# Mamba block of a fused graph network: six chunks of four tiles and one of two, with the first head in two halves

## The chip, the cores and the metric

The kernel runs on one core of a Trainium2 chip. The metric is the device time of one launch in microseconds (us). The engines are named as the profile names them: PE multiplies matrices (PEld is its weight load), DVE is VectorE, ACT is ScalarE, POOL is GpSimd, and SP issues DMAs.

## The reference

Four graph layers follow each other on 3327 nodes of 256 features, each with a residual and a layer norm. Layer 1 is the one that changes:

```python
h = relu(adj @ x @ gcn_w + gcn_b);  h = (h - mu) * rsqrt(var + EPS) * ln_g + ln_b
xz = h @ w_in;  xc, z = xz[:, :512], xz[:, 512:]
xconv = sum(xpad[k:k + L] * conv_w[:, k] for k in range(4)) + conv_b
u = silu(xconv);  dbc = u @ w_xp
dt = softplus(dbc[:, :16] @ w_dt + b_dt);  B = dbc[:, 16:32];  C = dbc[:, 32:]
dA = exp(dt[:, :, None] * A);  dBu = dt[:, :, None] * B[:, None, :] * u[:, :, None]
hst = dA[t] * hst + dBu[t];  ys[t] = hst @ C[t]      # a scan over the nodes, 512 channels x 16 states
out = ((ys + u * D_skip) * silu(z)) @ w_out
x = layernorm(x + out)
```

## The kernel before

The 3327 nodes are padded to 26 tiles of 128. Layer 0 comes first, then layer 1 (the Mamba block, some 350 to 1383 us of the profile), then layers 2 and 3, which the change leaves alone.

In the Mamba block, channels lie on partitions in four groups `g` (`NG`), and nodes run along the free dimension. The nodes are cut into chunks; `ends` and `starts` (from L263) hold their bounds. They are 3, 4, 4, 4, 4, 4 and 3 tiles, that is 384 columns in the first and last chunk and 512 in the others. Three streams of work are interleaved.

**Convolution.** `convolve` (L326) is a generator over the 26 tiles. A tile takes 26 matmuls against adjacency blocks loaded by SP (L340, L341), then a tail: ACT copies the sum to `m` (L349), PE transposes it (L352), ACT copies again (L354), PE multiplies by `gcn_w` (L357, L358), ACT applies relu (L361) and sums squares (L318), POOL makes the scale (L322 to L324), ACT applies it (`norm`, L368), PE turns the tile (`turn`, L378), and ACT writes it into `hT` (L380). A new tile's sum lies in the PSUM buffer `cb`, of which there is one, or for tiles 2, 4 and 6 in `y3`. `pump(tiles)` runs the generator until so many tiles are done.

**Head of a chunk.** The class `Head` (L483) makes what the scans read. `project` multiplies `hT` by `w_in` (L497), copies to `xc` (L499) and starts `u` (L500); `taps` adds three shifted products on DVE (L507); then `silu`, `mixed` (the product with `w_sp`, L521, whose rows B and C go to DRAM as `bc`, L526), `step_size` (L535 to L537), `exponentials`, `rounding`, `logarithms` and `finish`, which leaves dt and `du` (L560). A change between silu, exp and ln reloads ACT's table (`table_of`). `last` hands the last three columns from one head to the next.

**Scans.** For each chunk there are 16 slots, one for each state `s`. A slot takes, for each of four groups, a decay `dA` (ACT, two PSUM buffers, L600) and a scan (DVE, L615); then `product` (DVE, `hc`, two buffers) with the row C, and `add_up` (PE transposes into the accumulators `y0` to `y3`, L632), which is issued in the next slot. `feed` (POOL, L608) fills the next input of the scan from `du` and row B. `row` (L592) loads both rows from `bc`. Once `pinned` is set, DVE and POOL keep the program's order, and ACT's decays and table changes stand in one chain (`in_turn`, L289); the profile books DVE and POOL instructions of that part at L282, the line of the wrapper. The rest of PE's and ACT's work is placed by a scheduler, which prefers what stands under `tc.high_priority()`.

The head of chunk c + 1 and the output of chunk c - 1 are spread over the slots of chunk c: `plan(c)` gives the slot of each step, with slots of its own for chunk 0. The output is `gate` (DVE), `gated` (L643, L645) and `residual` (L656 to L661). `quota` sets how many units of convolution a slot may take. It spreads the tiles of chunk n evenly between two due times, by `duty`, an estimate of the slot's other PE work, and keeps `AHEAD` units in hand. In chunk 0 it gives nothing before slot 8. When all tiles are convolved, `values` prepares layer 2 in the same places: `value` transposes a finished tile (L460), copies it (L462), multiplies it by `wg` (L466) and writes `col` (L467) and `F` (L469, L470).

Before the slots stand `pump(3)`, the whole first head at 384 columns, and `pump(7)`. After the slots comes a tail over the last chunk's three tiles: add up, gate, transpose, `w_out` (L654), norm (L811), and their `value`. Layer 2 starts with a maximum over `col` (L923).

Of the kernel before, what the change touches and what calls it, by code (L numbers as in the profile page):

```python
# [18 lines left out]
P = 128  # L19
# [7 lines left out]
AHEAD = 96  # L27
SPLIT = 54
WC = 512
# [18 lines left out]
def gnn_kernel(ctx: ExitStack, tc: tile.TileContext, n: int, a: dict, out: bass.AP):  # L48
# [107 lines left out]
    with tc.tile_pool(name="l1b", bufs=1) as wpool, tc.tile_pool(name="l1at", bufs=2) as l1at:  # L156
# [35 lines left out]
        with tc.tile_pool(name="l1aw", bufs=1) as cwork, tc.tile_pool(name="l1c", bufs=2) as ch, \  # L192
# [61 lines left out]
            def plan(c):  # L254


                if c == 0:
                    return dict(project={g + 1: (g,) for g in range(NG)}, taps={7: (0,), 8: (1,), 9: (2, 3)}, gates={5: (0, 1), 6: (2,)},
                                silu=9, mixed=10, sizes={10: (0, 1), 11: (2, 3)}, exps=(11, 12), log=13)
                return dict(project={5: (0, 1), 6: (2, 3)}, taps={7: (0, 1), 8: (2, 3)}, gates={7: (0, 1), 8: (2, 3)},  # L260
                            silu=8, mixed=9, sizes={9: (0,), 10: (1, 2), 11: (3,)}, exps=(11, 12), log=13)

            ends = []  # L263
            while not ends or ends[-1] < npad:
                prev = ends[-1] if ends else 0
                ends.append(min(npad, prev + min(WC, (3 + len(ends)) * P)))
# [37 lines left out]
            banks = {0: ["y0", "y1", "y2", "ps"], 1: ["y3", "ps"]}  # L304
# [21 lines left out]
            def convolve():  # L326
# [3 lines left out]
                for it in range(nt):  # L330
                    if it < ends[1] // P and it % 2 == 0 and it:
                        cb = ypsum.tile([P, DI], F32, name="y3")
                    else:
                        cb = cpsum.tile([P, DI], F32, name="cb")
# [90 lines left out]
            def due(c):  # L425
                return c * DS + min(plan(c)["project"]) if c else 8
# [3 lines left out]
            def quota(c, s):  # L430


                k = c * DS + s
                n = next((x for x in range(2, nch) if k < due(x - 1)), None)
                if n is None:
                    return 24
                if k < due(0):
                    return 0
                if n not in shares:
                    busy = [duty(*divmod(i, DS)) for i in range(due(n - 2), due(n - 1))]  # L440
                    more = TILE * tiles_of(n)
                    level = max(busy) + more
                    while sum(max(0, level - x) for x in busy) > more:
                        level -= 1
                    shares[n] = [max(0, level - x) for x in busy]
                return TILE * starts[n] // P + sum(shares[n][:k - due(n - 2) + 1]) + AHEAD - taken
# [36 lines left out]
            class Head:  # L483

                def __init__(self, c):
                    self.c, self.w = c, ends[c] - starts[c]

                def project(self, g):

                    c, w = self.c, self.w  # L490
                    if g == 0:
                        self.xc = scratch()
                        gps.tensor_copy(self.xc[:, :, :3], last)
                        us[c] = ch.tile([P, NG, WC], F32, name="u", bufs=1)[:, :, :w]
                    ps = bank(self.c)
                    for k in range(2):
                        ten.matmul(ps[:, :w], w_in[:, k, g * P:(g + 1) * P], hTs[c][:, k, :w],  # L497
                                   start=(k == 0), stop=(k == 1))
                    act.copy(self.xc[:, g, 3:3 + w], ps[:, :w])  # L499
                    act.activation(us[c][:, g, :], self.xc[:, g, 0:w], AF.Identity, scale=conv_w[:, g, 0:1],  # L500
                                   bias=conv_b[:, g:g + 1])

                def taps(self, g):

                    u, w = us[self.c][:, g, :], self.w
                    for k in range(1, 4):
                        vec.scalar_tensor_tensor(u, self.xc[:, g, k:k + w], conv_w[:, g, k:k + 1], u,  # L507
                                                 op0=ALU.mult, op1=ALU.add)
                    if g == NG - 1:
                        gps.tensor_copy(last, self.xc[:, :, w:w + 3])  # L510

                def silu(self):
                    in_turn(act.activation, us[self.c], us[self.c], AF.Silu)

                def mixed(self):

                    c, w = self.c, self.w
                    m = w_sp.shape[2]
                    ps = bank(self.c)
                    for g in range(NG):  # L520
                        ten.matmul(ps[:m, :w], w_sp[:, g, :], us[c][:, g, :], start=(g == 0), stop=(g == NG - 1))  # L521
                    self.left = tmp.tile([P, WC], F32, name="gt", bufs=1)[:m, :w]
                    act.copy(self.left, ps[:m, :w])
                    bc = rows_of[c] = l1d.tile([2, DS, w], F32, name=f"bc{c}")
                    for k in range(2):
                        nc.sync.dma_start(bc[k], self.left[32 * k + DTR:32 * k + DTR + DS])  # L526
# [12 lines left out]
                def exponentials(self, g):  # L539

                    if g == 0:
                        self.e1 = scratch()[:, :, :self.w]
# [11 lines left out]
                def finish(self):  # L554

                    c, w, e1 = self.c, self.w, self.e1
                    vec.tensor_sub(e1, e1, self.e)
                    vec.scalar_tensor_tensor(e1, self.v, 0.0, e1, op0=ALU.max, op1=ALU.add)
                    du = ch.tile([P, NG, WC], F32, name="du", bufs=1)[:, :, :w]
                    vec.tensor_mul(du, e1, us[c])  # L560
                    xs[c] = e1, du
# [101 lines left out]
            pump(ends[0] // P)  # L663
            xs, ys = {}, {}
            first = Head(0)
            with tc.high_priority():
                for g in range(NG):
                    first.project(g)
                    first.taps(g)
                first.silu()  # L670
                table_of(AF.Exp)
                first.mixed()
                for g in range(NG):
                    first.step_size(g)
                for g in (0, 2):
                    first.exponentials(g)
                table_of(AF.Ln)
                first.rounding()
                first.logarithms()
                table_of(AF.Exp)  # L680
                first.finish()
            pump(ends[1] // P)
# [10 lines left out]
            for k, (c, s) in enumerate(states):  # L693
# [8 lines left out]
                if added:  # L702
                    with tc.high_priority() if s == 0 or c == 0 else nullcontext():
# [16 lines left out]
                if s == 0:  # L720
                    ys[c] = [ypsum.tile([P, DI], F32, name=f"y{i}") for i in range(m)]
                    with tc.high_priority() if c == 0 else nullcontext():
                        add_up(ys[c], us[c], first=True)
# [42 lines left out]
                if after:  # L766
                    if s == min(p["project"]):
                        pump(ends[c + 1] // P)
                    first = [lambda g=g: ahead.project(g) for g in p["project"].get(s, ())]
                    if s == p["mixed"]:  # L770
                        first += [ahead.mixed]
                    first += [lambda g=g: ahead.step_size(g) for g in p["sizes"].get(s, ())]
                    if c:
                        uses += first
                    else:
                        with tc.high_priority():
                            for use in first:
                                use()
# [844 lines left out]
```

## Time and profile before

| | us |
|---|---|
| three runs | 3509.28, 3515.73, 3515.77; median 3515.73 |
| the profiled execution | 3512.67, of which its span 3510.8 |
| chunk 0, from its first scan (436.60) to that of chunk 1 | 141.2 |
| chunks 1, 2, 3, 4 | 139.7, 139.4, 140.1, 138.9 |
| chunk 5, chunk 6 | 130.9, 95.2 |
| from the end of chunk 6's last scan (1361.95) to the maximum over `col` | 21.4 |

Times inside the profile are counted from the span's start. A line of an order of time gives start, length, engine, line of the kernel, operation, output and input with their shapes, and a count of merged instructions; the bracket at its end is the engine's idle time ahead of it and what ended that. A line of waits gives the waiting engine and tile, the releaser, the total in us, how many times, and the longest.

### The profile page before, as it was taken

The numbers are of one execution on the slowest core, as the hardware profiler recorded it, in microseconds if no ns is written. First come the engines' busy times: TensorE is split into PE (matmuls) and PEld (weight loads), VectorE is DVE, ScalarE is ACT, GpSimd is POOL, SyncE is SP. The second block draws the span as 40 slices with busy tenths as digits, with TensorE's granted clock in tenths as the row PEclk, the third lists the DMA queues.
The fourth block names the chain that finished last, engine by engine and source line by source line (L and its number), as shares of the span: only waits on it lengthen the run. The fifth ranks groups of instructions, "written<-read, shape, count | busy, mean of one in ns | idle before, by whom it ended". The sixth has DMA issues, their size and how long they took to land. (4 is left out here: it accounts for less than half of the span.)

```text
span 3510.8 us, 42847 instructions
## 1 busy us (share of the span) xinstructions
PE 3228.0 (92%) x15415; PEld 2526.5 (72%) x15415; DVE 2374.3 (68%) x5256; ACT 1737.1 (49%) x2749; POOL 932.2 (27%) x942
## 2 busy tenths in 40 slices
PE   9999888988988776999899999999997999999996
PEld 5888766666676555888677878777785777777775
DVE  2111168999999997777444444545434999999996
ACT  1000456767767674111233333333336888888883
POOL 0000055656665653111100000000001233333332
PEclk9999999999999888999899999999999999999998
DMA  5443334433443222444221212121212122222220
GB/s 179 147 151 122 112 104 115 113 106 118 101 115 90 67 58 92 131 142 149 84 67 49 65 48 67 50 64 53 61 48 73 55 57 69 66 69 61 70 66 16
DMA packets 138323, 304.62 MB, mean 87 GB/s; under 512 B 19086, under 2 KB 58574, under 8 KB 137966
## 3 DMA queue, kind: packets, MB, share of 16 engines
q1 hardware_dynamic: 138094, 301.72, 29.0%
q8 instruction: 125, 2.05, 0.2%
q14 instruction: 104, 0.85, 0.1%
HBM read 291.01 MB, written 10.65 MB: 86 GB/s over the span
## 5 line engine op out<-in xcount | busy, mean ns | idle before, releaser
L282 POOL TENSOR_TENSOR h<-du,row 128x2048 f32<-128x2048 f32 (+1 forms) x110 | 465.6, 4233 | 344.5 <-DVE hc L282 252.1
L282 DVE TENSOR_TENSOR_SCAN h<-dA,carry,h 128x512 f32<-128x512 f32 (+1 forms) x384 | 449.0, 1221 | 18.6 <-ACT dA L289 18.5
L289 ACT ACTIVATE dA<-t,A_log 128x512 f32<-128x512 f32 (+1 forms) x448 | 292.5, 658 | 146.3 <-DVE h L282 144.8
L1099 PE MATMUL acc<-X,wt 128*128 128x256 f32 x1352 | 346.3, 393 | 10.6 <-ACT wt L1097 10.2
L1066 PE MATMUL acc<-F,at 128*128 128x256 f32 x1352 | 354.3, 387 | 0.9 <-ACT q L840 0.6
L1099 PE MATMUL acc<-G,wt 128*128 128x256 f32 x1352 | 336.9, 392 | 5.5 <-ACT wt L1030 5.1
L1099 PEld LDWEIGHTS acc<-X,wt 128*128 128x128 f32 x1352 | 244.6, 191 | 106.2 <-issue 41.3
L1066 PE MATMUL acc<-X,at 128*128 128x256 f32 x1352 | 308.4, 381 | 0.0
L975 PE MATMUL acc<-F,at 128*128 128x257 f32 x1352 | 304.9, 382 | 1.3 <-DMA U<-in_U 1.3
L341 PE MATMUL cb<-F,at 128*128 128x256 f32 x1196 | 294.1, 394 | 4.8 <-ACT hn L361 3.4
L1099 PEld LDWEIGHTS acc<-G,wt 128*128 128x128 f32 x1352 | 250.7, 193 | 65.8 <-ACT wt L1030 35.2
L1111 DVE MAX8 cand<-e 128x8 f32<-128x128 f32 x676 | 142.2, 279 | 229.6 <-ACT e L1052 218.0
L118 PE MATMUL acc<-xa,at 128*128 128x257 f32 x1352 | 294.7, 380 | 0.0
L1066 PEld LDWEIGHTS acc<-F,at 128*128 128x128 f32 x1352 | 238.2, 191 | 75.3 <-issue 50.2
L118 PEld LDWEIGHTS acc<-xa,at 128*128 128x128 f32 x1352 | 255.9, 189 | 38.3 <-issue 0.5
L1066 PEld LDWEIGHTS acc<-X,at 128*128 128x128 f32 x1352 | 252.9, 191 | 40.3 <-issue 8.3
L975 PEld LDWEIGHTS acc<-F,at 128*128 128x128 f32 x1352 | 254.5, 191 | 37.3 <-issue 1.5
L632 PE MATMUL y<-ident,hc 128*128 128x128 f32 x1664 | 236.9, 297 | 46.2 <-DVE hc L282 46.1
L632 PEld LDWEIGHTS y<-ident,hc 128*128 128x128 f32 x1664 | 210.3, 154 | 87.5 <-DVE hc L282 62.8
L341 PEld LDWEIGHTS cb<-F,at 128*128 128x128 f32 x1196 | 229.4, 198 | 54.4 <-issue 14.5
L282 DVE TENSOR_TENSOR hc<-h,row 128x2048 f32<-128x2048 f32 (+2 forms) x114 | 242.3, 2127 | 11.0 <-PE y L632 4.3
L1097 ACT COPY wt<-tp 128x512 f32<-128x512 f32 (+1 forms) x182 | 93.6, 557 | 312.1 <-PE tp L1095 311.9
(351 smaller groups left out, 5219.4 us busy)
## 6 DMA issues: line engine op xcount, KB each, us to landing
at<-in_adjT SPq DMA_DIRECT2D x104, 832.0 KB, 4.5
at<-in_adjT SPq DMA_DIRECT2D x260, 320.0 KB, 3.0
row<-bc SPq DMA_DIRECT2D x80, 512.0 KB, 5.0
at<-in_adjT SPq DMA_DIRECT2D x52, 576.0 KB, 4.1
at<-in_adjT SPq DMA_DIRECT2D x26, 512.0 KB, 3.6
row<-bc SPq DMA_DIRECT2D x32, 384.0 KB, 4.8
qd<-q SPq DMA_DIRECT2D x104, 32.0 KB, 1.9
q<-qd SPq DMA_DIRECT2D x52, 64.0 KB, 1.9
```

Of the source, the lines that this page charges most:

```text
L118: nc.tensor.matmul(acc, at[:, j, :], rhs[:, j0 + j, :], start=(j0 + j == 0), stop=(j0 + j == nt - 1))
L282: return lambda *x, **k: tc.keep_in_program_order(op(*x, **k))
L289: decays.append(op(*x, **k))
L341: ten.matmul(acc, at[:, j % JC, :], X0[:, j, :], start=(j == 0), stop=(j == nt - 1))
L632: x = ten.matmul(y[:, g * P:(g + 1) * P], h[:, g, i * P:(i + 1) * P], ident, is_transpose=True, start=(first and g == 0), stop=(last and g ...
L975: nc.tensor.matmul(acc, at[:, j, :], F[:, j0 + j, :], start=(j0 + j == 0), stop=(j0 + j == nt - 1))
L1066: nc.tensor.matmul(acc, at[:, j, :], rhs[:, j0 + j, :], start=(j0 + j == 0), stop=(j0 + j == nt - 1))
L1097: copy(wt[:, :m, :], pt[:, :m, :])
L1099: nc.tensor.matmul(acc, wt[:, j, :], rhs[:, j0 + j, :], start=(j0 + j == 0), stop=(j0 + j == nt - 1))
L1111: nc.vector.max(cand[:, s * 8:(s + 1) * 8], z[:, s * SEG:(s + 1) * SEG])
```

## The change

The chunks become six of four tiles and one of two. The first head is made in two halves of 256 columns: `Head` takes an offset `o` and a width, and writes its part of `u`, `rows_of`, dt and `du`. Each half follows the convolution of its two tiles. Six tiles and not seven are convolved before the slots (`FREE`); tiles 6 and 7 are given to the slots 0 to 5 of chunk 0 by `quota`. The steps of chunk 1's head and the gates of chunk 0 move to other slots. In chunk 0 these steps and most `add_up` calls lose their high priority, and the head of chunk 1 the PSUM banks of its own.

```diff
+FREE = 6
 def plan(c):
     if c == 0:
-        return dict(project={g + 1: (g,) for g in range(NG)}, taps={7: (0,), 8: (1,), 9: (2, 3)}, gates={5: (0, 1), 6: (2,)},
+        return dict(project={6: (0, 1), 7: (2, 3)}, taps={8: (0, 1), 9: (2, 3)}, gates={8: (0, 1), 9: (2, 3)},
                     silu=9, mixed=10, sizes={10: (0, 1), 11: (2, 3)}, exps=(11, 12), log=13)
...
-    ends.append(min(npad, prev + min(WC, (3 + len(ends)) * P)))
+    ends.append(min(npad, prev + WC))
-banks = {0: ["y0", "y1", "y2", "ps"], 1: ["y3", "ps"]}
+banks = {0: ["y0", "y1", "y2", "ps"]}
...
-        if it < ends[1] // P and it % 2 == 0 and it:
+        if it in (2, 4):
             cb = ypsum.tile([P, DI], F32, name="y3")
...
 def due(c):
-    return c * DS + min(plan(c)["project"]) if c else 8
+    return c * DS + min(plan(c)["project"])
 def quota(c, s):
     k = c * DS + s
-    n = next((x for x in range(2, nch) if k < due(x - 1)), None)
+    n = next((x for x in range(1, nch) if k < due(x - 1)), None)
     if n is None:
         return 24
-    if k < due(0):
-        return 0
+    begin, tiles = (due(n - 2), starts[n] // P) if n > 1 else (0, FREE)
     if n not in shares:
-        busy = [duty(*divmod(i, DS)) for i in range(due(n - 2), due(n - 1))]
-        more = TILE * tiles_of(n)
+        busy = [duty(*divmod(i, DS)) for i in range(begin, due(n - 1))]
+        more = TILE * (ends[n] // P - tiles)
...
-    return TILE * starts[n] // P + sum(shares[n][:k - due(n - 2) + 1]) + AHEAD - taken
+    return TILE * tiles + sum(shares[n][:k - begin + 1]) + AHEAD - taken
 class Head:
-    def __init__(self, c):
-        self.c, self.w = c, ends[c] - starts[c]
+    def __init__(self, c, o=0, w=None):
+        self.c, self.w, self.o = c, w or ends[c] - starts[c], o
+        self.all = ends[c] - starts[c]
+    def mine(self, x):
+        return x[:, :, self.o:self.o + self.w]
...
-pump(ends[0] // P)
 xs, ys = {}, {}
-first = Head(0)
-with tc.high_priority():
-    for g in range(NG):
-        first.project(g)
-        first.taps(g)
+for o in range(0, WC, WC // 2):
+    pump((o + WC // 2) // P)
+    first = Head(0, o, WC // 2)
+    with tc.high_priority():
+        for g in range(NG):
+            first.project(g)
+            first.taps(g)
...
-pump(ends[1] // P)
+pump(FREE)
...
-        with tc.high_priority() if s == 0 or c == 0 else nullcontext():
+        with tc.high_priority() if s == 0 else nullcontext():
             summed = add_up(*added)
...
-        with tc.high_priority() if c == 0 else nullcontext():
-            add_up(ys[c], us[c], first=True)
+        add_up(ys[c], us[c], first=True)
...
-        first = [lambda g=g: ahead.project(g) for g in p["project"].get(s, ())]
+        uses += [lambda g=g: ahead.project(g) for g in p["project"].get(s, ())]
         if s == p["mixed"]:
-            first += [ahead.mixed]
+            uses += [ahead.mixed]
-        first += [lambda g=g: ahead.step_size(g) for g in p["sizes"].get(s, ())]
-        if c:
-            uses += first
-        else:
-            with tc.high_priority():
-                for use in first:
-                    use()
+        uses += [lambda g=g: ahead.step_size(g) for g in p["sizes"].get(s, ())]
```

The methods of `Head` read and write through `self.u`, `self.mine(...)` and the offset `o`, and the half with `o == 0` allocates the tiles that both halves share.

## The prediction

> **What bounds the kernel now.** I read the page's slices first, then busy time by stage, then VectorE's waits and its order of time. The page has DVE at 9 tenths and PE at 8 to 9 in slices 5 to 15, the Mamba block. The table of busy time by stage, cut at the first scan of each chunk (columns: stretch, its length, then PE, PEld, DVE, ACT and POOL busy, granted clock, DMA share, GB/s), says which chunk is bound by what:
>
> ```profile
> 436.60:577.80 141.20, 116.68 (x544) 87.37 (x542) 103.96 (x97) 88.07 (x176) 68.08 (x36) 0.94 0.38 109
> 577.78:717.50 139.72, 124.00 (x604) 95.38 (x605) 132.09 (x100) 96.50 (x187) 89.77 (x35) 0.93 0.39 110
> ...
> 996.93:1135.84 138.91, 119.52 (x619) 91.68 (x617) 132.99 (x101) 95.69 (x182) 86.13 (x32) 0.96 0.37 102
> 1135.84:1266.70 130.86, 93.31 (x446) 71.78 (x446) 128.53 (x101) 95.28 (x203) 76.57 (x24) 0.84 0.27 63
> 1266.70:1361.95 95.25, 67.81 (x348) 52.82 (x348) 88.38 (x85) 64.63 (x166) 54.38 (x18) 0.86 0.24 58
> ```
>
> From chunk 1 on DVE is busy 93 to 98%: the scans set the pace. Chunk 0 is the exception: 37 of its 141.2 us are idle on DVE though it has only three tiles. DVE's order of time shows where the largest piece lies:
>
> ```profile
> 479.66 3.49 DVE L282 TENSOR_TENSOR_SCAN h<-dA,h 128x384 f32<-128x384 f32 x4
> 500.07 2.33 DVE L282 SCALAR_TENSOR_TENSOR u<-t,conv_w,u 128x512 f32<-128x512 f32 x3 [16.91 <-ACT u L500]
> ```
>
> The taps of chunk 1's head stand in slot 7 of chunk 0 and wait 16.9 us for the projection, which waits for tile 6 (its hT is done at 494.65). DVE's waits of this stretch add the rest:
>
> ```profile
> DVE h L282 <- ACT dA L289: 20.9, 8, 5.9
> DVE u L282 <- ACT u L500: 16.9, 1, 16.9
> ```
>
> **What the skill says.** The Trainium skill, "VectorE: DVE Perf Modes", section on the TRN2 errata, gives (N+151)/0.96 ns for an fp32 tensor_tensor. The trace agrees: 1.76 us at 1536 elements, 2.29 at 2048. For 1024 I take its 1.22 us, an estimate. "ScalarE: Activation LUTs", section What ACT_TABLE_LOAD costs, gives 1283 ns for a table load, and the trace has 1.28; a second head pays four of them again. Its further drain of 1380 ns is not seen: after the load at 410.98 the next ACTIVATE starts at 412.28. Its 280 + 0.833 N ns for an ACTIVATE fits dA (0.582 us at 384 columns, 0.688 at 512) within 4%; I take 0.48 at 256. "Perfetto Trace Analysis", Identifying the Most-Contended Engine, warns that matmul busy time is no measure of headroom: PE at 0.89 of a full chunk is PEld at 0.68, but PE still waits 15 us in each for ACT's copies, so I treat PE as nearly full.
>
> **The change, part by part.** The order of the changed program's instructions, engine by engine, was read beside that of before. Prices: a four-tile slot is 4.80 us of scans (0.06 less each without carry) and 2.29 of product, 7.1 us in cadence, 6.85 without carry; a convolution step (a 256-wide fp32 matmul) is two PE instructions at 0.22 us each (48 in 10.55), so a tile is 11.5 us and about 2 for its tail; the 16 transposes of a slot are 2.65 us (12 in 1.98).
>
> 1. *Start of the scans.* Now: hT of tile 2 at 399.86, Ln of the head ends at 429.28, du at 434.65, first scan 436.60. After: the first half starts behind tile 1 (hT 385.72) and puts 16 projection instructions (3.5 us), 8 of w_sp (1.8), 8 of w_dt (0.8) and a wait for hn behind the last table load (2.8) into PE's queue, ahead of tiles 2 and 3. By PE's order tile 2 is convolved at 397.7, tile 3 at 415.9, its hT (7.6 us later, as for tile 1) at 423.4. The second half at 256 columns takes 22.8 us from there to the end of Ln, against 29.4 at 384 (two thirds of the copies, step sizes and exponentials, and Ln is no longer behind tile 3's norm): 446.1. Three DVE instructions at 1.22: du at 449.9; the first quarter of the 512-wide POOL feed 1.3: **first scan at 451.4, +14.8 us.** The extra two bc writes (0.4 us each on SP) and the halves' copies of last on POOL hide under this chain; with their cover gone they cost 1 us.
>
> 2. *Chunk 0, four tiles.* Its own DVE work is 16 x 6.85 + 17.9 (12 taps at 0.75, four 2048-wide steps) = 127.5 us. PE has tile 5 done at 453.6, as scanning begins, and the order puts tile 6 whole ahead of the first slot's transposes, 7 and 8 ahead of the sixth's. PE: 5 + 21 matmuls and the turn of tile 5 bring it to 471.4, the first slot's transposes with tile 6's tail to 477.4. The products have two buffers, so slot 2's product, ready at 471.0, waits to 477.6: 6.5 us. After that PE and DVE go side by side to slot 7 (513 to 515), with 2.7 us more of such waits and 1.4 at the start. The projection follows in slots 6 and 7 and is done at about 519 and 527, before the taps at 521 and 531: **the 16.9 us wait is gone.** Slots 8 to 15 are taken from chunk 1 of now (74.3 us from slot 8's product to the end, 1.8 less without carry). Sum 147 us against 141.2: **+5.8**, for one tile more. SP's queue: row loads stand ahead of at loads and wait for a product; by the same walk each at load still lands before its matmul (tile 8's last third by 506, wanted at 508), so I cost them nothing; if cover fails, 4.1 us each.
>
> 3. *Chunks 1 to 4* keep shapes and pacing. Four residuals in chunk 1 and not three is what chunk 2 has now, in 139.4 us. Chunk 4 convolves two tiles and not three: **-1.**
>
> 4. *Chunk 5* prepares a 256-wide head: 12 taps 0.15 us less each and four steps 1.76 to 1.22: **-3.9.** The gates moved to slots 8 and 9 are PE and ACT work, under DVE.
>
> 5. *Chunk 6, two tiles.* DVE's own work falls from 16 x 5.5 + 2.4 to 16 x 3.9 (4 x 0.67 + 1.2) + 2.4 = 65 us. But ACT, 64.6 us busy there now, keeps 58 (64 dA shorter by 0.10, one sz copy and half the silu less, one `value` of 1.2 more), in an order that mixes `value`, residual and gt into dA, with just two dA buffers and scans of 0.67. One `value` goes L460, m, L466, col, F and was 4.7 us long from 1344.69, above a slot's 3.9. Such ACT work already stalls at 384 columns:
>
> ```profile
> 1359.93 1.93 DVE L282 TENSOR_TENSOR_SCAN h<-dA,carry,h 128x384 f32<-128x384 f32 x2 [1.90 <-ACT dA L289]
> ```
>
>    Bounds: 68 (DVE's work, all hidden) and 90 (5.6 a slot). I take 82, so **-13.2.**
>
> 6. *Tail.* From the last product (1361.95) to the maximum over col (1383.33) 21.4 us for three tiles; the second tile's col stands at 1378.19, and the first product starts the same. One tile less: **-5.3.**
>
> Sum: 14.8 + 5.8 - 1 - 3.9 - 13.2 - 5.3 = **-2.8 us**. Against the profiled execution's 3512.67 that is 3509.9; the median shown is 3.06 above it. I say 3512.0, a fall of 0.1% from 3515.73. All else (layer 0, layers 2 and 3) is untouched. A measurement of this kernel can tell about 0.2%, 7 us, from no change.
>
> **The rivals.**
> - *The short last chunk runs at DVE's pace*, and the wait at slot 2 is all that PE costs chunk 0. For it: chunk 5 now has 0.9 us of dA waits with the same values; ACT was busy 65 of chunk 6's 95 us. Against: the four-link chain of a `value`. Chunk 6 at 70 and chunk 0 at 145 give -17: 3499.
> - *PE becomes the bound of chunk 0.* Three tiles and seven slots' transposes are 61 us of PE work in the 62 us to slot 7, with PE unstalled. In chunks 1 to 4 PE is 89% busy at best, because each tile's tail waits for two ACT copies that now queue behind dA. At 89% the 61 become 69, the debt reaches the projection and moves the taps of slots 8 and 9: +8 us, and 4 more in chunk 1, whose slots 6 and 7 already wait 4.3 us for the transposes. That gives +9: 3525. It decides when the first slot's transposes end after about 482. Against: at 480 to 506 PE ran with the full clock and few waits.
> - *It doesn't do what it says:* the scheduler could leave tiles 6 and 7 where they were. The order of the changed program excludes that; chance 1 in 100.
>
> **How the numbers follow.** The sum as it stands, with 3 us either way for the start, 6 for chunk 0 and 6 for chunk 6, holds 0.42; the first rival and cases like it 0.31; PE as the bound and other slower cases 0.26; no change of order 0.01. The likeliest case alone spans 3506 to 3519. The unknown ends (chunk 6 from 68 to 90, chunk 0 from 145 to 159) carry the range to 3499 and 3527. Of the 0.42 some 0.08 fall under -7 us and 0.03 over +7; of the 0.31 some 0.28 are under -7; of the 0.26 some 0.23 are over +7. So: faster 0.36, same 0.38, slower 0.26.
>
> **What would show it.** Right: first scan near 451; no DVE wait for u in slot 7 and one wait of 5 to 8 us of a product for the transposes in slot 2; chunk 0 of 147 us, the last chunk near 82, col's maximum about 16 us after the last product. Wrong: DVE waits for transposes through slots 3 to 9 (PE binds), a last chunk under 74 with no dA waits (first rival), or a first scan after 456.

## The result, and the profile after

The changed kernel takes 3509.88 us (median of 12 runs, 3504.62 to 3513.86). In the same series the kernel before took 3511.91 (12 runs, 3509.22 to 3515.97), so the ratio is 0.9994, with a 95% interval of 0.9985 to 1.0002: no difference that can be told. The profiled execution took 3504.92 us (span 3503.0).

The busy time by stage, cut at the first scan of each chunk as before (columns: stretch, its length, then PE, PEld, DVE, ACT and POOL busy, granted clock, DMA share, GB/s). The stretches are chunks 0, 1, 4, 5 and 6 and the tail up to the maximum over `col`; chunk 6 ends, here and before, with the start of the last product, 0.1 us behind the last scan:

```profile
452.13:606.29 154.16, 132.00 (x646) 100.61 (x645) 128.73 (x97) 95.42 (x180) 87.80 (x36) 0.94 0.42 115
606.29:746.90 140.61, 121.82 (x608) 92.89 (x607) 132.56 (x101) 98.20 (x190) 87.43 (x35) 0.95 0.38 109
...
1026.70:1167.41 140.71, 111.74 (x563) 84.94 (x561) 132.75 (x102) 95.35 (x180) 83.76 (x29) 0.89 0.35 89
1167.41:1295.31 127.90, 85.39 (x438) 67.10 (x438) 124.53 (x102) 90.19 (x195) 73.44 (x24) 0.87 0.25 62
1295.31:1368.70 73.39, 56.82 (x290) 42.53 (x290) 65.28 (x85) 54.84 (x164) 37.56 (x18) 0.90 0.25 51
1368.70:1383.16 14.46, 10.46 (x45) 7.04 (x44) 5.06 (x19) 5.18 (x17) 2.12 (x6) 0.92 0.00 1
```

The first scan starts 15.5 us later than before (452.13 for 436.60). Chunk 0 is 13.0 us longer (154.2 for 141.2): DVE has 24.8 us more work in it (128.73 for 103.96), and its idle time falls only from 37 to 25 us. Chunks 1 to 5 together are 0.1 longer (689.0 for 688.9), chunk 6 is 21.8 shorter (73.4 for 95.2) and the tail 6.9 shorter (14.5 for 21.4). The sum is -0.1: the maximum over `col` starts at 1383.16, where it started at 1383.33. The change moves nearly 29 us from the end of the block to its front.

The profiled spans do differ, by 7.8 us, but behind the block, where the code is the same. From that maximum to the end of the span the profiled executions of the 14 kernels took 2119.8 (the changed kernel) to 2128.6 us (the third experiment), with 2127.5 for the kernel before. I take this for scatter between executions: the 12 runs of the changed kernel alone spread over 9 us. With one profile of each kernel it isn't shown that none of it belongs to the change.

DVE's waits in chunk 0 after (what waited, for what; us in total, times, longest), and below them the scans, products and taps of its order of time that matter (start, length, what it is, and in brackets the idle time ahead of it):

```profile
DVE h L283 <- ACT dA L290: 16.7, 6, 6.4
DVE hc L283 <- PE y L641: 7.4, 2, 7.0
DVE h L283 <- POOL h L617: 1.4, 1, 1.4
```

```profile
482.14 2.29 DVE L283 TENSOR_TENSOR hc<-h,row 128x2048 f32<-128x2048 f32 x1 [7.04 <-PE y L641]
...
524.45 4.63 DVE L283 SCALAR_TENSOR_TENSOR u<-t,conv_w,u 128x512 f32<-128x512 f32 x6
...
565.22 1.22 DVE L283 TENSOR_TENSOR_SCAN h<-dA,h 128x512 f32<-128x512 f32 x1 [6.40 <-ACT dA L290]
567.58 1.22 DVE L283 TENSOR_TENSOR_SCAN h<-dA,h 128x512 f32<-128x512 f32 x1 [1.14 <-ACT dA L290]
...
587.27 2.34 DVE L283 TENSOR_TENSOR_SCAN h<-dA,h 128x512 f32<-128x512 f32 x2 [4.82 <-ACT dA L290]
```

The taps at 524.45 have no wait: the 16.9 us for `u` are gone. In their place stand a wait of slot 2's product for the transposes (7.0) and three late waits of the scans for `dA`, 12.4 us together: two in slot 12 and one in slot 14, counted from 0 by the scans. (The expectations below call them slots 11 and 13.)

In the last chunk the longest wait for `dA` is this one, in the last slot:

```profile
1367.21 1.39 DVE L283 TENSOR_TENSOR_SCAN h<-dA,carry,h 128x256 f32<-128x256 f32 x2 [3.09 <-ACT dA L290]
```

All seven waits of chunk 6 come to 6.6 us, and DVE is busy 65.3 of its 73.4 us: the short last chunk runs at nearly DVE's own pace.

### The profile page after: what moved, and what is told of

Its sections match the earlier page's. It is cut to its first block, busy times and chain, and to the rows that moved or that the text cites. A ratio compares the mean times of both kernels' runs of the same rounds, so it can differ in the third digit from the quotient of the medians.

```text
span 3503.0 us, 42964 instructions
## 1 busy us (share of the span) xinstructions
PE 3216.6 (92%) x15449; PEld 2518.7 (72%) x15449; DVE 2375.9 (68%) x5268; ACT 1746.5 (50%) x2784; POOL 927.3 (26%) x941
## 5 line engine op out<-in xcount | busy, mean ns | idle before, releaser
L283 DVE TENSOR_TENSOR_SCAN h<-dA,carry,h 128x512 f32<-128x512 f32 (+1 forms) x384 | 432.3, 1176 | 22.5 <-ACT dA L290 22.1
L342 PE MATMUL cb<-F,at 128*128 128x256 f32 x1248 | 308.0, 395 | 6.0 <-ACT hn L362 3.0
L342 PEld LDWEIGHTS cb<-F,at 128*128 128x128 f32 x1248 | 239.3, 198 | 57.3 <-issue 13.3
L283 DVE TENSOR_TENSOR hc<-h,row 128x2048 f32<-128x2048 f32 (+2 forms) x113 | 243.7, 2158 | 14.5 <-PE y L641 7.8
```

The costliest lines, as they stand in the source:

```text
L283: return lambda *x, **k: tc.keep_in_program_order(op(*x, **k))
L342: ten.matmul(acc, at[:, j % JC, :], X0[:, j, :], start=(j == 0), stop=(j == nt - 1))
```

## The experiments

Theory A: the new sizes gain nearly 29 us at the end and cost more than that at the start; the pacing and the halves bring some of it back, and the change has these effects cancel. The rivals give the gain or the loss to another part. Stages below are from one profiled execution each, in us; the tail ends at the maximum over `col`. The ratio is to the kernel before on the same chip. Between the series that kernel's median went from 3509.4 to 3513.0, so the ratio decides and not the bare time.

| kernel | first scan | chunk 0 | chunks 1-5 | chunk 6 | tail | end of block | ratio (95%) |
|---|---|---|---|---|---|---|---|
| before | 436.6 | 141.2 | 688.9 | 95.2 | 21.4 | 1383.3 | 1 |
| changed | 452.1 | 154.2 | 689.0 | 73.4 | 14.5 | 1383.2 | 0.9994 (0.9985-1.0002) |
| 1 new sizes only | 463.9 | 158.2 | 690.6 | 73.9 | 15.3 | 1402.0 | 1.0055 (1.0042-1.0068) |
| 2 pacing only | 437.8 | 128.1 | 688.8 | 95.2 | 21.4 | 1371.3 | 0.9961 (0.9947-0.9974) |
| 3 changed, whole head | 464.3 | 147.0 | 688.9 | 74.1 | 15.2 | 1389.5 | 1.0009 (1.0001-1.0017) |
| 4 changed, one plan | 450.9 | 149.6 | 686.2 | 74.2 | 15.2 | 1376.1 | 0.9971 (0.9960-0.9983) |
| 5 changed, transposes first | 450.9 | 174.0 | 689.7 | 73.7 | 15.4 | 1403.8 | 1.0046 (1.0032-1.0060) |
| 6 changed, exponentials later | 450.4 | 153.9 | 687.6 | 74.1 | 15.2 | 1381.3 | 0.9990 (0.9983-0.9997) |
| 7 as 2, one plan | 436.7 | 130.6 | 687.8 | 95.3 | 21.4 | 1371.8 | 0.9959 (0.9946-0.9973) |
| 8 as 4, five tiles ahead | 452.0 | 153.1 | 686.5 | 74.1 | 15.2 | 1380.8 | 0.9978 (0.9969-0.9987) |
| 9 changed, step sizes ahead | 451.9 | 162.5 | 687.0 | 73.7 | 15.4 | 1390.5 | 1.0000 (0.9990-1.0010) |
| 10 as 2, two tiles first | 412.8 | 131.4 | 695.2 | 116.5 | 24.0 | 1379.9 | 0.9994 (0.9986-1.0002) |
| 11 as 2, step sizes ahead | 436.6 | 126.8 | 689.1 | 95.3 | 21.4 | 1369.2 | 0.9959 (0.9944-0.9973) |
| 12 as 2, head in two parts | 434.8 | 135.7 | 689.2 | 95.4 | 21.5 | 1376.5 | 0.9961 (0.9947-0.9975) |

### 1 and 2: the sizes alone, and the pacing alone

The first takes the kernel before with the new sizes; `gates` has to name the fourth tile, and the head of chunk 1 loses a PSUM bank, `y3`, that chunk 0 now needs for its fourth tile:

```diff
-                    ... gates={5: (0, 1), 6: (2,)},
+                    ... gates={5: (0, 1), 6: (2, 3)},
-                ends.append(min(npad, prev + min(WC, (3 + len(ends)) * P)))
+                ends.append(min(npad, prev + WC))
-            banks = {0: ["y0", "y1", "y2", "ps"], 1: ["y3", "ps"]}
+            banks = {0: ["y0", "y1", "y2", "ps"]}
```

> The kernel before with the new chunk sizes alone (six of four tiles and one of two; the first head whole, all eight tiles of chunks 0 and 1 asked for ahead of the scans, no convolution in chunk 0 before slot 8). Theory A (the new sizes gain some 29 us at the end, the last chunk -22 and the tail -7, and pay for it at the start; halves and pacing only keep the price down): first scan near 457 (head behind tile 3, 512 wide), a DVE wait for u in chunk 0's slot 7 of 17 us or more, chunk 0 of 160 to 170, chunk 6 of 73, tail 14 to 15; total +10 to +25 against the kernel before. Rival B (the sizes decide, halves and pacing carry nothing): within 3 us of the changed kernel in every stage, total -2 to +3.

The second takes the changed kernel back to the old sizes and the whole head. What is left of the change is called the pacing here: tiles convolved in chunk 0's slots, its new plan, the lower priorities and the bank. `FREE` goes down by one with the first chunk, so that two tiles still fall into the slots:

```diff
-FREE = 6
+FREE = 5
-                ends.append(min(npad, prev + WC))
+                ends.append(min(npad, prev + min(WC, (3 + len(ends)) * P)))
-            for o in range(0, WC, WC // 2):
-                pump((o + WC // 2) // P)
-                first = Head(0, o, WC // 2)
+            for o in (0,):
+                pump(ends[0] // P)
+                first = Head(0)
```

> The changed kernel with the old chunk sizes (three tiles, five times four, three) and one whole first head of three tiles; five tiles are convolved ahead of the scans and tiles 5 and 6 in chunk 0's slots. Theory A: first scan at 436 to 438, chunk 6 and tail as before (95 and 21), no wait for u in slot 7 but some 5 to 10 us of waits for the transposes and the step sizes in its place: chunk 0 of 128 to 138, total -3 to -13 against the kernel before, so that the pacing alone is worth about what the whole change was hoped to bring. Rival C (chunk 0 is bound by PE, and pacing only moves the wait): chunk 0 of 139 to 145, total within 3 us of before.

The sizes alone cost 0.55%, 19 us. The end gains nearly what it gains in the changed kernel (21.4 in chunk 6, 6.1 in the tail), and the front loses 44.3: 27.3 before the first scan (20 were expected) and 17.0 in chunk 0 (158.2, just under the 160 to 170 expected). The pacing alone gains 0.39%, 14 us: chunk 0 falls from 141.2 to 128.1, and no other stage moves by more than 1.2. DVE's waits in chunk 0, first with the sizes alone, then with the pacing alone:

```profile
DVE h L282 <- ACT dA L289: 23.9, 7, 17.9
```

```profile
DVE h L283 <- ACT dA L290: 20.2, 14, 7.5
DVE hc L283 <- PE y L641: 6.7, 5, 1.9
```

With the sizes alone I had looked for a wait for `u` of 17 us or more. It is 1.0 us, and one of 17.9 for `dA` comes later. With eight tiles convolved in front the projection is in time. But from 554 to 568 us ACT's order holds the four step sizes, each of which waits 1.0 to 1.4 us for PE, and after them the tail of a tile, ahead of the `dA` that DVE needs. All four go through the one bank `ps` there, where the kernel before had `y3` too. How much of the 19 us is the lost bank was not measured. With the pacing alone the wait for `u` is gone too, and 6.7 us for transposes come, as the theory said. Rivals B and C fall.

### 3 and 12: the halves

The third is the changed kernel with the three lines of the whole head, as in the second. The last experiment is the second's kernel with its first head in parts of two tiles and one:

```diff
-            for o in (0,):
-                pump(ends[0] // P)
-                first = Head(0)
+            for o, part in ((0, 2 * P), (2 * P, P)):
+                pump((o + part) // P)
+                first = Head(0, o, part)
```

> The changed kernel with its first head whole, 512 wide, behind tile 3, and not in two halves. Theory A (the first half's work in PE's, ACT's and DVE's queues costs little, and the second half is shorter): first scan at 455 to 460 against 452.1, chunk 0 within 3 of 154.2, total +3 to +8 against the changed kernel. Rival D (the first half stands ahead of tiles 2 and 3 on PE, and four more table loads, so halves gain nothing): first scan at 446 to 452, total 0 to -6 against the changed kernel.

> The second experiment's kernel (old sizes, pacing) with its first head in two parts, two tiles and one, so that only sizes differ from the changed kernel besides the part widths. Theory A (halves start the scans earlier, and the first part's work on PE and ACT delays tile 2 and is paid back in chunk 0 as waits for the transposes, as between the changed kernel and the third experiment, where 12.2 us at the start became 7.2 us more of chunk 0): first scan at 431 to 435 against 437.8, chunk 0 of 129 to 134 against 128.1, total 0 to -4 against the second experiment's 3497.5. Rival D (with one tile in the second part, halves gain nothing: hT of tile 2 comes some 10 us later than with the whole head, and that eats the narrower part): first scan at 436 to 441, total +1 to +6.

With the new sizes the whole head starts the scans at 464.3, 12.2 us later than the halves (I had expected 3 to 8), but chunk 0 is then 7.2 shorter, where I had expected no change over 3: by its first scan the trace has 323 of PE's convolution matmuls, and the changed kernel 298 by its own. A tile has 52, so PE is half a tile further, and DVE waits for no transposes in slot 2. Theory A holds in sign and in sum, not in its parts. Net the halves are worth 6.3 us to the block, and 0.15% in the ratios. With the old sizes the parts gain 3.0 at the start and lose 7.6 in chunk 0, where this wait appears:

```profile
463.50 1.76 DVE L283 TENSOR_TENSOR hc<-h,row 128x1536 f32<-128x1536 f32 x1 [9.47 <-PE y L641]
```

In the profiled executions the block grows by 5.2. The ratios of the second and the last experiment are equal (0.9961), so nothing can be told between them in time; chunk 0 at 135.7 was over what was expected (129 to 134). What an earlier start gains there, PE's unfinished convolution takes back.

Both pairs give the price of the sizes with pacing: 1.0009 against 0.9961 with the whole head, 0.9994 against 0.9961 with parts, that is 17 and 12 us.

### 4 and 6: why chunk 0 waits for dA

The fourth deletes chunk 0's own plan, so that it follows the others', with the gates and the head's steps from the projection to the first step sizes a slot earlier. The sixth moves only the first exponential, from slot 11 to 12:

```diff
-                if c == 0:
-                    return dict(project={6: (0, 1), 7: (2, 3)}, taps={8: (0, 1), 9: (2, 3)}, gates={8: (0, 1), 9: (2, 3)},
-                                silu=9, mixed=10, sizes={10: (0, 1), 11: (2, 3)}, exps=(11, 12), log=13)
```

```diff
-  ... sizes={10: (0, 1), 11: (2, 3)}, exps=(11, 12), log=13)
+  ... sizes={10: (0, 1), 11: (2, 3)}, exps=(12, 12), log=13)
-                        ahead.exponentials(2 * p["exps"].index(s))
+                        [ahead.exponentials(2 * i) for i in range(2) if p["exps"][i] == s]
```

> The changed kernel with chunk 0 following the plan of the other chunks (projection in slots 5 and 6, taps in 7 and 8, silu 8, mixed 9, step sizes in 9 to 11: all one slot earlier, the exponentials where they were). Theory E (the 12 us of DVE waits for dA in slots 10 to 15 of chunk 0 come from the one slot less that step sizes have before the exponentials): these waits fall to 4 or less as in chunks 1 to 4, chunk 0 of 143 to 148, total -6 to -11 against the changed kernel. Rival F (PE has no room: tiles 6 and 7 are not done by slot 5): a wait for u of 5 to 10 us in slot 7 takes their place and longer waits for the transposes come in slots 2 to 5; chunk 0 of 152 to 160, total within 4 of the changed kernel.

> The changed kernel with both exponentials of chunk 1's head in slot 12 of chunk 0 (they were in 11 and 12), all else the same: the step sizes have a slot more, and nothing is earlier on PE. Theory E (in chunk 0 the exponentials stand in ACT's queue before their step sizes are there, and the dA behind them are late): the 6.4 us wait at 565 in slot 11 falls to 2 or less, while the 4.8 us of slot 13 (both exponentials and the logarithms now close together) stays or grows by up to 2; chunk 0 of 148 to 152, total -3 to -6 against the changed kernel. Rival I (these dA are late because ACT has too much to do there): the wait moves to the next slot whole, chunk 0 within 1 of 154.2, total within 2.

The fourth, chunk 0's waits:

```profile
DVE hc L280 <- PE y L638: 10.4, 5, 7.2
DVE h L280 <- ACT dA L287: 10.3, 6, 3.6
```

The late waits are 3.6 in slot 12 and 1.1 in slot 13 where the changed kernel had 7.5 in slot 12 and 4.8 in slot 14, while PE, asked for tiles 6 and 7 a slot sooner, holds the products up by 3.0 more. Chunk 0 falls by 4.6, chunk 1 by 2.0, the block by 7.1, the ratio from 0.9994 to 0.9971. So most of the late waits hang on chunk 0's own plan; the gain in chunk 0 was less than theory E said (6 to 11), and rival F's price was paid too, in part. No wait for `u` appears. But theory E's reason, too little room for the step sizes ahead of the exponentials, can account for slot 12 alone, where 2.9 us went if slot 13 is counted in. The 4.8 us of slot 14, which went whole, have another reason, shown below.

The sixth, two scans:

```profile
557.58 1.22 DVE L283 TENSOR_TENSOR_SCAN h<-dA,h 128x512 f32<-128x512 f32 x1 [0.30 <-ACT dA L290]
...
571.48 2.34 DVE L283 TENSOR_TENSOR_SCAN h<-dA,h 128x512 f32<-128x512 f32 x2 [8.05 <-ACT dA L290]
```

The wait of slot 12 goes and one of 8.05 comes in slot 13. Chunk 0 stays within 0.3, as rival I said. It is not the place of the exponentials. ACT's order in the changed kernel shows what its queue holds while DVE waits in slot 12 for the `dA` at 564.50:

```profile
556.79 0.69 ACT L543 ACTIVATE t<-ps,b_dt 128x512 f32<-128x512 f32 x1 [1.21 <-PE ps L542]
557.38 0.68 ACT L544 ACTIVATE t<-ps,b_dt 128x512 f32<-128x512 f32 x1
559.52 0.69 ACT L543 ACTIVATE t<-ps,b_dt 128x512 f32<-128x512 f32 x1 [1.46 <-PE ps L542]
560.11 0.68 ACT L544 ACTIVATE t<-ps,b_dt 128x512 f32<-128x512 f32 x1
560.82 2.15 ACT L290 ACTIVATE t<-t 128x1024 f32<-128x1024 f32 x2
562.87 0.67 ACT L543 ACTIVATE t<-ps,b_dt 128x512 f32<-128x512 f32 x1
563.44 0.68 ACT L544 ACTIVATE t<-ps,b_dt 128x512 f32<-128x512 f32 x1
564.01 0.59 ACT L290 ACTIVATE hn<-hn,nb,rs 128x256 f32<-128x256 f32 x1
564.50 0.69 ACT L290 ACTIVATE dA<-t,A_log 128x512 f32<-128x512 f32 x1
```

Three step sizes, the exponentials and a tile's norm, 7.7 us from 556.79 to 564.50, of it 1.46 of waiting for the second step size on PE; all of it stands ahead of a `dA` that DVE needs.

The wait in slot 14 looks alike in DVE's rows, but ACT is idle for most of it. POOL's and then ACT's order at that place:

```profile
580.33 4.52 POOL L283 TENSOR_TENSOR h<-du,row 128x2048 f32<-128x2048 f32 x1 [4.48 <-DVE hc L283]
584.93 0.19 POOL L283 TENSOR_SCALAR rs<-sq 128x1 f32<-128x1 f32 x1
```

```profile
586.06 0.60 ACT L290 ACTIVATE hn<-hn,nb,rs 128x256 f32<-128x256 f32 x1 [3.94 <-POOL nb L283]
586.57 1.28 ACT L290 ACTIVATE dA<-t,A_log 128x512 f32<-128x512 f32 x2
```

The norm of a convolved tile stands ahead of the `dA` in ACT's order and waits 3.94 us for its scale. POOL makes that scale behind the feed of the next scan, as the program's order has it, though its input was there at 577.4 and POOL stood idle from 575.9 to 580.3, waiting for a product. The same wait, 4.8 to 4.9 us, stands in slot 14 of experiments 3, 5, 6 and 9, each time with ACT waiting 2.7 to 4.0 us for `nb`; none of these touches it. In the fourth that tile's scale comes ahead of the feed (574.58, with the feed at 580.02), and the wait is gone. No run moved the scale alone, so this is read from the order of the instructions and was not tested by itself.

### 5, 8 and 9: PE's order in chunk 0

The fifth restores high priority for chunk 0's transposes. The eighth is the fourth's kernel with `FREE = 5`. The ninth gives `mixed` and the step sizes high priority in chunk 0 (their calls are made at once under `tc.high_priority()`, and not put into `uses`).

```diff
-                    with tc.high_priority() if s == 0 else nullcontext():
+                    with tc.high_priority() if s == 0 or c == 0 else nullcontext():
                         summed = add_up(*added)
```

```diff
-FREE = 6
+FREE = 5
```

```diff
+                    sizes = []
                     if s == p["mixed"]:
-                        uses += [ahead.mixed]
-                    uses += [lambda g=g: ahead.step_size(g) for g in p["sizes"].get(s, ())]
+                        sizes = [ahead.mixed]
+                    sizes += [lambda g=g: ahead.step_size(g) for g in p["sizes"].get(s, ())]
+                    if c:
+                        uses += sizes
+                    else:
+                        with tc.high_priority():
+                            for use in sizes:
+                                use()
```

> The changed kernel with the transposes of chunk 0's products at high priority again, as before the change: the first slot's transposes go ahead of tile 6 on PE. Theory G (slot 2's wait of 7.0 us is only a matter of order on PE): the wait falls under 1 us and nothing comes in its place, chunk 0 of 146 to 148, total -5 to -8 against the changed kernel. Rival H (PE has no room up to slot 8, the wait is PE's debt): tiles 6 and 7 are finished later by as much, and the wait comes back as one for u before the taps of slots 8 and 9, or as waits for dA behind the projection; chunk 0 of 152 to 158, total within 3 of the changed kernel.

> The fourth experiment's kernel (new sizes, two halves, chunk 0 on the plan of the other chunks) with five tiles ahead of the scans and not six, so that tile 5 too is convolved in chunk 0's slots and the first slots' transposes are not behind tile 6. Theory G (slot 2's wait of 7.2 us is only order): chunk 0 of 143 to 147 against 149.6, total -3 to -6 against the fourth. Rival H (PE's debt): three tiles of 11.5 us, five slots of 16 transposes and the projection are 60 us of PE work in the 50 us to slot 7, so a wait for u or for the transposes of 5 to 12 us comes in slots 5 to 8; chunk 0 of 150 to 158, total 0 to +9 against the fourth.

> The changed kernel with the w_sp matmuls and step sizes of chunk 1's head at high priority in chunk 0, as before the change, so that they go ahead of the convolution on PE; the projection and the transposes stay paced. Theory J (the late dA waits of 6.4, 1.1 and 4.8 us come from convolution steps that stand between the four step sizes on PE, while ACT waits for a step size with dA behind it): these waits fall from 12.4 to 6 or less, chunk 0 of 146 to 150, total -4 to -8 against the changed kernel. Rival K (they come from the one ps bank and ACT's own queue: the next step size can't start before ACT has read the last, and ACT reads it behind dA): they stay at 10 to 13, chunk 0 of 152 to 156, total within 3.

None of the three gains on the kernel it starts from. In the fifth the wait of slot 2's product is gone, as theory G had it, but chunk 0 grows by 20 us, far more than even rival H allowed. DVE's waits, and ACT's and DVE's order of time around the longest wait but one:

```profile
DVE h L283 <- ACT dA L290: 35.6, 8, 9.6
DVE u L283 <- ACT u L506: 6.8, 2, 5.3
```

```profile
480.77 0.37 ACT L350 COPY m<-cb 128x256 f32<-128x256 f32 x1 [6.59 <-PE cb L342]
481.72 0.37 ACT L355 COPY m<-cb 128x256 f32<-128x256 f32 x1 [0.58 <-PE cb L353]
483.43 0.38 ACT L362 ACTIVATE hn<-cb 128x256 f32<-128x256 f32 x1 [1.33 <-PE cb L359]
...
485.98 0.60 ACT L290 ACTIVATE hn<-hn,nb,rs 128x256 f32<-128x256 f32 x1 [1.21 <-POOL nb L283]
486.49 1.28 ACT L290 ACTIVATE dA<-t,A_log 128x512 f32<-128x512 f32 x2
```

```profile
487.19 2.34 DVE L283 TENSOR_TENSOR_SCAN h<-dA,h 128x512 f32<-128x512 f32 x2 [9.27 <-ACT dA L290]
```

ACT's queue holds the tail of tile 6 ahead of the next slot's `dA`. With the transposes first, PE finishes that tile later, ACT waits 6.6 us for it and then goes through the tail, and the `dA` comes 9.3 us late. The same happens with tile 7 in slot 6 (6.2 us). So here PE's debt reaches DVE through ACT's queue, and at more than its own size: the 7.0 us of slot 2 are gone, and chunk 0 is 19.8 longer.

In the eighth the wait of slot 2's product is spread over those of slots 3 and 4 (4.6 and 3.2) and one of 5.6 for `dA` follows in slot 5; chunk 0 loses 3.5 against the fourth, inside rival H's span. The ratios can't tell the two apart (0.9978 against 0.9971). In the ninth the `dA` waits of chunk 0 grow from 16.7 to 21.7 and those for transposes from 7.4 to 10.7. Theory J falls; chunk 0 (162.5) is longer than rival K had it. The profiled blocks differ by 7.3 us, the ratios (1.0000 against 0.9994) by 2, so its price is 0 to 7 us.

### 7, 10 and 11: can the pacing alone be bettered?

The seventh deletes chunk 0's plan in the second's kernel (as the fourth does), the eleventh puts its step sizes ahead (as the ninth does), and the tenth turns the sizes round, two tiles first and four last:

```diff
-                ends.append(min(npad, prev + min(WC, (3 + len(ends)) * P)))
+                ends.append(min(npad, prev + (WC if ends else 2 * P)))
```

> The second experiment's kernel (old chunk sizes, whole first head of three tiles, pacing) with chunk 0 following the plan of the other chunks. Theory E: the late dA waits of chunk 0 (7.5 us in slot 11 and some smaller ones) fall by 5 to 8 us, chunk 0 of 120 to 124 against 128.1, total -4 to -8 against the second experiment, so about 3490 to 3494: faster than any kernel here. Rival F (PE has no room: five tiles are done when scanning begins, and tiles 5 and 6 must be done a slot earlier): a wait for u in slot 7 or longer waits for the transposes take their place, chunk 0 of 127 to 132, total within 3 of the second experiment.

> The second experiment's kernel (whole first head, pacing, five tiles ahead) with chunk sizes two and six times four: the mirror image of the change. Theory A (a tile that leaves the first chunk starts the scans earlier but adds to the last chunk and the tail, and PE's convolution of the tiles of chunk 1 bounds chunk 0): first scan at 414 to 420, a wait for u in chunk 0's slot 7 or waits for transposes of 15 us and more, chunk 0 of 105 to 115, chunk 6 of 114 to 120, tail of 27 to 29; total within 7 of the second experiment's 3497.5, so still faster than before. Rival L (chunk 0 runs at DVE's pace, as its start decides): chunk 0 of 85 to 95, total -12 to -20 against the second experiment.

> The second experiment's kernel (old sizes, pacing) with the w_sp matmuls and step sizes of chunk 1's head at high priority in chunk 0. Theory J: the late dA wait of 7.5 us in slot 11 falls to 2 or less, chunk 0 of 121 to 124 against 128.1, total -3 to -7 against the second experiment's 3497.5. Rival K: it stays or moves to the next slots, chunk 0 of 127 to 130, total within 3.

The seventh and the eleventh can't be told from the second (0.9959, 0.9959, 0.9961). In the seventh the waits change owner: with one plan, those for `dA` in chunk 0 fall from 20.2 to 16.0 and those for transposes rise from 6.7 to 9.6, as rival F had it. In the eleventh they are 13.8 and 9.8: the wait of 7.5 falls to 3.2, those for `dA` by 6.4 in all, but 3.1 came for transposes, and chunk 0 gained 1.3, not 4 to 7.

The tenth starts to scan 25 us earlier and loses it at once:

```profile
451.84 1.23 DVE L283 TENSOR_TENSOR hc<-h,row 128x1024 f32<-128x1024 f32 x1 [27.49 <-PE y L641]
```

```profile
412.83:544.27 131.44, 114.83 (x501) 86.11 (x500) 81.94 (x97) 79.09 (x178) 49.85 (x36) 0.91 0.37 109
```

PE still has tiles 3 to 5 to convolve, so DVE is busy 82 of 131 us. Rival L (85 to 95) falls; chunk 0 was longer than theory A's 105 to 115 too, because I had looked for the PE wait in slot 7 and smaller. The tail is 24.0, where 27 to 29 were expected. Its total is 12 us over the second's by the ratios (0.9994 against 0.9961), outside the 7 expected, and so not told apart from the kernel before.

## Why the prediction was right, and where its steps were wrong

No change to speak of was the forecast (3512.0, a sum of -2.8 us), and -2.0 came. But the steps were less good than their sum, and that the sum held is luck: two errors of 7 to 9 us, of opposite sign, cancelled, and inside one of them a slip in counting hid 7 us more (step 2).

1. *Start of the scans*, +14.8 predicted, **+15.5** measured. Right, by its own chain: `hT` of tile 3 at 424.9 (423.4 predicted), the end of Ln at 446.9 (446.1), the last wait 1.4 us for POOL's feed (1.3).
2. *Chunk 0*, +5.8 predicted, **+13.0** measured. The wait of slot 2 was right (6.5 to 477.6 predicted; 7.0 to 482.1 measured), and so was the end of the wait for `u`. Slot 8's product began at 529.0, 3.1 later than predicted, 0.7 of it from the start; two early waits for `dA` (2.4 and 1.3) that the walk had not were in part made up by waits for transposes that it had and that did not come. The step that failed is "Slots 8 to 15 are taken from chunk 1 of now", and it failed twice. First, the 74.3 us start at this product of chunk 1:

```profile
638.76 4.54 DVE L282 SCALAR_TENSOR_TENSOR u<-t,conv_w,u 128x512 f32<-128x512 f32 x6
643.21 2.28 DVE L282 TENSOR_TENSOR hc<-h,row 128x2048 f32<-128x2048 f32 x1
```

   It follows the first taps, as slot 8's product does in chunk 0 of the changed kernel. But chunk 1's plan has its first taps in slot 7, so this is slot 7's product, and the 74.3 us hold one slot too many (7.1). Without it the step is some 65 us and the chunk 140, a fall of 1; the whole sum would have been about -10. Second, from slot 8's product to the end it was 77.3 us, some 12 over that 65, and these are the 12.4 of late waits for `dA`, of which chunk 1 of now has 1.4 in its last slots. So the prediction put at next to nothing a wait of 12 us, and the slot counted too often covered 7 of it. Chunk 0's plan has the head's last steps closer together than chunk 1's, and the kernel before had such waits in its own chunk 0 (4.2, 3.4 and 5.9 in slots 10, 11 and 14, of the 20.9 us in the view that I showed): I took the wrong chunk as the model. In the fourth experiment, with one plan for all, 7.7 of the 12.4 us go, 4.8 of them the wait for POOL's scale.
3. *Chunks 1 to 4*, -1 predicted, **+3.1** measured (chunk 1 +0.9, chunks 2 and 3 +0.4, chunk 4 +1.8). PE's work in chunk 4 did fall, from 119.5 to 111.7 us, but it was cover and not bound, DVE being busy for 133 us of 139, and the step should have been costed at nothing; its waits for `dA` rose from 3.1 to 4.7 us.
4. *Chunk 5*, -3.9 predicted, **-3.0** measured.
5. *Chunk 6*, -13.2 predicted, **-21.8** measured; the first rival was nearer (70 us, against 73.4 measured). DVE's own work was right (65 predicted, 65.3 measured). The failing step is that a `value` of 4.7 us, set against a slot of 3.9, would hold the `dA`. There is no `value` in every slot: the chunk has 13 in 16 slots, before and after, and 13 of 4.7 us are 61, less than DVE's 65. Nor does one hold the queue: in the changed kernel the copies that open a `value` (L462) come at 1313.04, 1319.35, 1325.18, 1331.47, and `dA` goes between its links. ACT's idle time for them in chunk 6 is 6.1 us (1.8 and 4.3 ahead of L462 and L467), and DVE waits 6.6 in all. A chain of latencies is a bound only if what stands behind it in that queue waits, and DVE's waits for `dA` in chunk 6 of before (5.6 us) already said that little did.
6. *Tail*, -5.3 predicted, **-6.9** measured. The last tile's share was 4.6 (`col` at 1378.19 and 1382.77 before). The rest is that after the last product the second tile's `col` came in 13.9 us and not in the 16.2 of before.

The rival that PE binds chunk 0 was half right. Waits for transposes through slots 3 to 9 did not come (0.4 us), and the product of slot 2 began right at its point of decision, 482. It had chunk 0 at 155 us, near the 154.2 measured, but not by its mechanism: what was lost beyond the sum in slots 12 and 14 are waits for `dA` behind the head's last steps and a tile's norm in ACT's order.

The four parts of the change that the experiments can price: the pacing is worth 14 us by itself (0.9961). The sizes cost 19 us without pacing, 12 to 17 with it. The halves bring back some 5 us with the new sizes and nothing with the old ones. Chunk 0's own plan, whose last steps the change left as they were, costs 8 us with the new sizes (0.9994 against 0.9971) and nothing with the old ones (0.9961 against 0.9959). So the second experiment, the change without its sizes and halves, beats both kernels by 0.3 to 0.4%.

What stays open: which of the two, ACT's load there or the step sizes on PE, sets the `dA` waits of slot 12, since moving either alone (6 and 9) did not take them away; whether slot 14's wait goes when POOL makes the scale ahead of the feed; what the priorities and the banks are worth apart; and whether the eleventh's 1.3 us in chunk 0 are real.

## What to carry to other kernels

Moving work from the last stage to the first is no gain in itself: at the end it saves its own time, at the start it waits for its inputs, so cost the first result's delay ahead of the saving. Where work stands in one order, a step that waits for a late producer holds up everything behind it, and the delay is then booked to another engine. Here ACT waited 6.6 us for PE in the fifth experiment and 3.9 for POOL in the changed kernel, and DVE's rows named `dA` both times; follow such a wait one engine further before you give it a cause. To cost a stage whose size changes, take as model the stage with the same plan and not the one with the same size, and count its slots from the plan.

## What the runs showed of the hardware

In these rows DVE's product and POOL's work hold each other up, and DVE's scans and POOL's work don't. In chunk 0 of the changed kernel, DVE:

```profile
502.99 2.29 DVE L283 TENSOR_TENSOR hc<-h,row 128x2048 f32<-128x2048 f32 x1
505.19 4.62 DVE L283 TENSOR_TENSOR_SCAN h<-dA,h 128x512 f32<-128x512 f32 x4
509.90 2.97 DVE L283 TENSOR_TENSOR hc<-h,row 128x2048 f32<-128x2048 f32 x1
```

and POOL at the same time:

```profile
503.17 2.15 POOL L283 TENSOR_SCALAR rs<-sq 128x1 f32<-128x1 f32 x1
505.41 0.55 POOL L283 TENSOR_TENSOR rs<-rs,mhalf 128x1 f32<-128x1 f32 x1
506.04 0.19 POOL L283 TENSOR_TENSOR nb<-nm,rs 128x1 f32<-128x1 f32 x1
506.18 4.55 POOL L283 TENSOR_TENSOR h<-du,row 128x2048 f32<-128x2048 f32 x1
```

An operation on one column that takes 0.19 us at 524.63 in the kernel before takes 2.15 here and ends with DVE's product (505.3). The next product begins under POOL's feed, which ends at 510.73, and takes 0.68 us longer than its 2.29. The scans beside the same feed keep their time: 4.62 us for four. The Trainium skill, "Trainium Architecture — The Big Picture", section What this means for kernel authors, names this pair as the only engines that contend in SBUF, by an exclusive lock; these rows agree for the product, and the scans show no such loss. Both inputs of the product lie in SBUF, while one input of the scan, `dA`, lies in PSUM; whether that makes the difference no run tested. All three products of chunk 0 that took 2.6 to 3.1 us began under a feed of POOL.
